# Grouping the numerators of a product-quantised convolution behind its denominators, on one Trainium2 core

## The chip, the cores and the metric

The kernel runs on one core of one Trainium2 chip. The metric is the device time of one execution in microseconds. All times in this text are microseconds unless ns is written. The engines are named as in the profile: PE is TensorE (the matmul array), PEld its weight loads, DVE is VectorE, ACT is ScalarE, POOL is GpSimd, SP is SyncE, which here only issues transfers.

## What is computed

The input x is 16 images of 256 channels, 28 by 28, in fp32. A group norm is followed by two convolutions of 3x3 that are replaced by soft lookups, then by a squeeze-and-excite gate and two residual sums. Cut to what matters:

```python
def amm_conv3x3(x, centroids, w_sub):                  # centroids: (C, 16, 9)
    p = patches_of_3x3(x)                              # B, N, C, 9
    d = sum(p*p) - 2*einsum('bncs,cks->bnck', p, centroids) + sum(centroids**2)
    attn = softmax(-d, axis=-1)                        # over the 16 codes of a channel
    lut = einsum('cks,cso->cko', centroids, w_sub)
    return einsum('bnck,cko->bno', attn, lut)

h = relu(bn1(amm_conv3x3(gn(x), centroids1, wsub1)))   # layer 1
h = bn2(amm_conv3x3(h, centroids2, wsub2))             # layer 2
h = relu(se_layer(h) + gn(x))
return x + h
```

For each pixel and each channel there are 16 logits, a softmax over them, and a weighted sum. The kernel rearranges the sum: it first forms, for each channel and each of the nine taps, the attention-weighted centroid (the numerator, a matmul of the exponentials with the centroids), divides by the sum of the exponentials (the denominator), and multiplies the result q with w_sub (the lookup).

## The kernel before

**Blocks.** An image in one layer is cut into four blocks: two halves of the channels (hh) times two halves of the rows (t), in the order of `BLOCKS`. There are 16 images, 2 layers and so 128 blocks. Block j has four groups of 32 channels, mm = 0 to 3, and 392 pixels.

**What a block does.** `patches` brings nine shifted copies of the padded image from DRAM into one of two tiles `pt`. `logits` (L349) is a matmul in 32x32 tiles of the array, 16 per group mm, into four PSUM banks `lg`; `exps` (L361) takes the exponential of each bank on ScalarE into a tile `e`. `num_b` (L410) makes the denominators and the ninth tap together, in tiles of 64 rows by 32 columns, into two banks `nb`. `split_b` (L421, L423, ScalarE) and `join_b` (L430, L433, VectorE) separate them, `recip_dve` (L436) inverts the denominators, and `spread` (L447, L451) shuffles them to the rows where they are needed, into tiles `rb`. `num_a` (L396) makes the other eight taps, a pair of taps and two banks `na` for each mm. Pairs 0 and 1 are copied out by ScalarE (`copy_a`, L464) and multiplied later by GpSimd (`scale_q`, L459); pairs 2 and 3 are multiplied straight out of PSUM by VectorE (`scale_a`, L470). The ninth tap (the tile `qo`, spread number 4) is scaled by GpSimd as well.

**Lookups.** The lookup of an image is a product of two-by-two blocks (two channel halves in, two out, two row halves), done with seven products instead of eight, in the way of Strassen's scheme. `PRODUCTS` says in which cluster each product runs and with which taps: `KO` is the order of the nine taps, `S1` is split over two clusters. `product` (L478) adds nine 128x128 matmuls into one bank `acc`. The differences of q that the scheme needs are made by GpSimd in `mix` (L485, L487); `acc_copy`, `acc_add` and `reg_add` (L509, L515, L517, L522) put the seven sums together, `norm_out` (L529, L533) applies the batch norm on ScalarE.

**Wide blocks.** In layer 2, blocks of channel half 0 treat their group mm = 0 with a softmax that subtracts the maximum: `wide_copy` (ScalarE, L367), `wide_turn` (a VectorE transpose and a maximum, L372 and L375), `wide_sub` (GpSimd, L381), `wide_back` (VectorE, L385), `wide_exp` (ScalarE, L389).

**The order.** Nothing is left to a scheduler: `at(cl, sub, f, ...)` puts a step into a list under a cluster number and a fraction, and the steps are issued in the order of these two keys; steps under one key go in the order in which they were put. Each engine executes its own steps in that order. Block j has g = 2j. Its logits of mm 0 and 1 are in cluster g, those of mm 2 and 3 in g+1, its denominators in g+2; an image has g = 8n and takes eight clusters. Below, cluster numbers are often taken modulo 8. In an even cluster TensorE does two logits groups of one block, the denominators and numerators 0 and 1 of the block before, and then a lookup (2.0); in an odd cluster two logits groups, numerators 2 and 3, and a lookup.

**Buffers.** PSUM is one ring of eight banks of 2 KiB, shared by all of `lg`, `nb`, `na`, `acc` and a few small sums. An allocation waits until a bank is free. A lookup input lives in one of the tiles `qp` (pairs) or `qo` (ninth taps), whose numbers `NQ` sets and whose use is planned in the list `homes`.

**Other steps that are touched.** Before the first block, channels 0 to 127 and then 128 to 255 of image 0 are normalised (`gn_stats`, `gn_mean`, `gn_var`, `gn_apply`), written to DRAM with `to_home1`, and the codes of layer 1 are centred (`center`: squares by `center_sq`, a matmul and a sum by `center_add`, the subtraction of a mean by `center_mean`). The codes of layer 2 are centred in the same way in clusters 43 to 51 by `prep_wd2` (three parts), `prep_wd3` and `prep_wd4`. `finish_norm`, `finish_gate`, `finish_sum`, `finish_relu` and `finish_add` finish an image of layer 2 in later clusters (3, 4 and 5 of the image after the next).

Of the kernel before, what the change touches and what calls it, by code (L numbers as in the profile page):

```python
# [37 lines left out]
NQ = {"pair": 14, "one": 4}  # L38
# [4 lines left out]
    5: ("A11", 0, KO), 6: ("S1", 0, KO[:3]), 7: ("S1", 0, KO[3:]), 8: ("S3", 1, KO), 9: ("S2", 0, KO),  # L43
# [24 lines left out]
def kernel(  # L68
# [180 lines left out]
    def center_sq(wf, c0, w):  # L249
        sq = rpool.tile([P, N], F32, tag="r", name="sq")  # L250
        nc.vector.tensor_mul(sq[:, :w], wf[:, c0 : c0 + w], wf[:, c0 : c0 + w])
        return sq
# [6 lines left out]
    def center_mean(wf, n):  # L259
        g = wf.rearrange("p (g k) -> p g k", k=K)  # L260
        nc.vector.tensor_reduce(cst[:, : n // K], g, axis=AX.X, op=ALU.add)
        nc.vector.tensor_scalar_mul(cst[:, : n // K], cst[:, : n // K], 1.0 / K)
        nc.vector.tensor_sub(g, g, cst[:, : n // K].unsqueeze(2).to_broadcast([P, n // K, K]))
# [180 lines left out]
    def spread(u, mm):  # L444
        if mm == 4:
            rb = rpool.tile([P, N], F32, tag="rb1", name="rb1", bufs=1)
            nc.vector.stream_shuffle(rb, u["r"], mask_of(8))  # L447
        else:
            rb = rpool.tile([P, 2, N], F32, tag="rb", name="rb", bufs=4)
            for r in range(2):  # L450
                nc.vector.stream_shuffle(rb[:, r, :], u["r"], mask_of(2 * mm + r))  # L451
        u["rb", mm] = rb
# [222 lines left out]
    def prep_wd2(part):  # L675
        pw["sq"] = center_sq(pw["st"][:, 512:1536], 384 * part, min(384, 1024 - 384 * part))
# [4 lines left out]
    def prep_wd4():  # L681
        st = pw.pop("st")
        center_mean(st[:, 512:1536], 1024)
        f = st[:, 512:1536].rearrange("p (g n) -> p g n", n=32)
        nc.vector.tensor_sub(f, f, kbias.unsqueeze(1).to_broadcast([P, 32, 32]))
# [157 lines left out]
    for j, u in enumerate(blocks):  # L843
        gi, g = 8 * (j // 4), 2 * j
        for mm in range(5):
            kind = "one" if mm == 4 else "pair"
            homes.append(((g + 3, 1.1) if 2 <= mm < 4 else (g + 2, 1.4), 1, j, mm, kind))
# [8 lines left out]
    for j, u in enumerate(blocks):  # L856
# [21 lines left out]
        at(g + 2, 1.7, spread, u, 4)  # L878
        at(g + 2, 1.71, scale_q, u, 4)
        for mm in range(2):  # L880
            at(g + 2, 1.35, num_a, u, mm)
            at(g + 2, 1.45, copy_a, u, mm)
            at(g + 3, 1.8, spread, u, mm)
            at(g + 3, 1.8, scale_q, u, mm)
        for mm in range(2, 4):
            at(*((g + 2, 1.8) if mm == 2 else (g + 3, 0.05)), spread, u, mm)
            at(g + 3, 1.0, num_a, u, mm)
            at(g + 3, 1.1, scale_a, u, mm)

    for l in range(2):  # L890
        for b in range(B):
# [3 lines left out]
            for c, (w, r, ks) in PRODUCTS.items():  # L895
                at(g + c, 2.0, product, (n, c), us[r], w, ks)
# [6 lines left out]
            at(g + 6, 0.0, acc_copy, l, b, c11, (n, 5))  # L903
# [14 lines left out]
            if l == 0:  # L918
# [8 lines left out]
                if b + 1 < B:  # L927
                    at(g + (-1 if b else 2), 2.6, load_x, b + 1)
                    for q in range(NB):
                        at(g + (1 + 2 * q if b else 4), 0.3, gn_stats, b + 1, q)  # L930
                    at(g + 4, 1.05 if b else 1.96, gn_mean, b + 1)
                    at(g + 4, 1.33 if b else 1.97, gn_var, b + 1)
                    for q in range(NB):
                        at(g + 5, 0.9, gn_apply, b + 1, q)
                        at(g + 5, 1.9, to_home1, b + 1, q)
# [20 lines left out]
    at(1, 0.6, load_w, 0, "A11")  # L956
    at(3, 0.6, load_w, 0, "S3")
    at(3, 0.6, load_w, 0, "A22")
# [27 lines left out]
    at(51, 0.3, prep_wd4)  # L986
# [20 lines left out]
    for k in range(NB):  # L1007
# [4 lines left out]
        if k == 0:  # L1012
            for i in range(2):
                to_home1(0, 0, i)
            nc.vector.memset(pts[0], 1.0)
            nc.gpsimd.memset(pts[1], 1.0)
    for hh in range(2):
        center(wts["wd", hh].rearrange("p a b c -> p (a b c)"), 512)
    at(-0.5, 0.7, to_home1, 0, 1)
    at(0, 1.95, setup_bn)  # L1020
# [160 lines left out]
```

## Time and profile before

| what | value |
|---|---|
| median of three runs | 2773.61 (2771.26 to 2779.5) |
| profiled execution | 2760.28 |
| its span, as the page counts it | 2758.7 |
| mean granted TensorE clock | 0.987 |
| PE busy | 2674.9 (97%) |
| DVE, ACT, POOL busy | 1732.6, 1454.4, 2066.8 |
| logits L349, matmuls | 533.5 |
| numerators L396, denominators L410 | 412.1, 372.2 |
| lookups L478 from `qp` | 709.0 and 521.3 |
| mixes on POOL, L487 | 938.2 |
| POOL's own scaling, L459 pairs | 473.0 |

The busy times of the page say which engine is occupied. A busy PE is not the same as an array that streams rows: in the timeline, the start of one group of matmuls minus the start of the next shows what a group really costs. In the lists of waits, a line names who waited, for whom, the total, how often, and the longest. In a timeline a line has the start, the duration, the engine, the line of the kernel, the operation, output and inputs, and how many instructions were merged; in square brackets stands the idle time of the engine before it and what ended it.

### The profile page before, as it was taken

The numbers are of one execution on the slowest core, as the hardware profiler recorded it, in microseconds if no ns is written. First come the engines' busy times: TensorE is split into PE (matmuls) and PEld (weight loads), VectorE is DVE, ScalarE is ACT, GpSimd is POOL, SyncE is SP. The second block draws the span as 40 slices with busy tenths as digits, with TensorE's granted clock in tenths as the row PEclk, the third lists the DMA queues.
The fourth block names the chain that finished last, engine by engine and source line by source line (L and its number), as shares of the span: only waits on it lengthen the run. The fifth ranks groups of instructions, "written<-read, shape, count | busy, mean of one in ns | idle before, by whom it ended". The sixth has DMA issues, their size and how long they took to land. (4 is left out here: it accounts for less than half of the span.)

```text
span 2758.7 us, 87946 instructions
## 1 busy us (share of the span) xinstructions
PE 2674.9 (97%) x37076; PEld 1297.7 (47%) x37076; DVE 1732.6 (63%) x3950; ACT 1454.4 (53%) x3277; POOL 2066.8 (75%) x1420
## 2 busy tenths in 40 slices
PE   5989999799999999999999999999999999999997
PEld 2444444344444444444444444444444444444443
DVE  5765555765555565565576766676766666766664
ACT  4444455445455445455455466656566656556653
POOL 4756787738877767766678777888877788877787
PEclk9999999999999999999999999999999999999998
DMA  9665677546677656666585455445555545555541
GB/s 202 149 135 136 165 191 184 146 107 158 154 189 189 157 128 151 158 160 150 117 183 122 105 123 122 111 104 114 114 123 123 115 104 113 116 117 123 117 105 47
DMA packets 223025, 374.51 MB, mean 136 GB/s; under 512 B 30152, under 2 KB 193336, under 8 KB 222624
## 3 DMA queue, kind: packets, MB, share of 16 engines
q1 hardware_dynamic: 215392, 334.50, 53.8%
q0 software_dynamic: 7232, 34.30, 3.6%
q8 instruction: 296, 4.85, 0.8%
q14 instruction: 105, 0.86, 0.1%
HBM read 288.91 MB, written 79.80 MB: 134 GB/s over the span
## 5 line engine op out<-in xcount | busy, mean ns | idle before, releaser
L361 ACT ACTIVATE e<-lg 128x392 f32<-128x392 f32 x1920 | 777.7, 530 | 822.7 <-PE lg L349 821.7
L487 POOL TENSOR_TENSOR qp<-qp,qp 128x784 f32<-128x784 f32 x512 | 938.2, 1862 | 41.8 <-DVE qp L470 41.8
L478 PE MATMUL acc<-qp,w_S 128*128 128x392 f32 x2048 | 709.0, 497 | 5.3 <-POOL qp L487 5.2
L459 POOL TENSOR_TENSOR qp<-qp,rb 128x784 f32<-128x784 f32 x256 | 473.0, 1869 | 253.6 <-DVE rb L451 253.6
L349 PE MATMUL lg<-pt,wd 32*32 32x392 f32 x16384 | 533.5, 503 | 28.8 <-DVE half_sum L515 17.3
L451 DVE STREAM_SHUFFLE rb<-r 128x392 f32<-128x392 f32 x1024 | 550.8, 605 | 0.0
L478 PEld LDWEIGHTS acc<-qp,w_S 128*128 128x128 f32 x2048 | 388.5, 191 | 296.7 <-POOL qp L487 10.9
L478 PE MATMUL acc<-qp,w_A 128*128 128x392 f32 x1536 | 521.3, 493 | 0.0
L396 PE MATMUL na<-e,cwa 64*32 64x392 f32 x8192 | 412.1, 498 | 10.0 <-issue 9.8
L430 DVE SCALAR_TENSOR_TENSOR r<-nb,kst,r 128x392 f32<-128x392 f32 x128 | 79.8, 624 | 517.5 <-ACT r L421 510.6
L478 PEld LDWEIGHTS acc<-qp,w_A 128*128 128x128 f32 x1536 | 292.5, 190 | 213.1
L410 PE MATMUL nb<-e,cwb 64*32 64x392 f32 x8192 | 372.2, 497 | 0.0
L349 PEld LDWEIGHTS lg<-pt,wd 32*32 32x32 f32 x16384 | 230.9, 103 | 282.8 <-issue 179.6
L436 DVE RECIPROCAL r<-r 128x392 f32<-128x392 f32 x128 | 331.9, 2593 | 0.0
L459 POOL TENSOR_TENSOR qo<-qo,rb 128x392 f32<-128x392 f32 x128 | 131.1, 1024 | 220.3 <-DVE rb L447 220.2
L470 DVE TENSOR_TENSOR qp<-na,rb 128x392 f32<-128x392 f32 x512 | 252.4, 555 | 56.1 <-PE na L396 53.1
L396 PEld LDWEIGHTS na<-e,cwa 64*32 64x32 f32 x8192 | 145.2, 106 | 234.6 <-ACT e L361 123.5
L410 PEld LDWEIGHTS nb<-e,cwb 64*32 64x32 f32 x8192 | 146.2, 107 | 209.2 <-issue 126.5
L464 ACT COPY qp<-na 128x392 f32<-128x392 f32 x512 | 211.8, 512 | 10.9 <-PE na L396 10.8
L421 ACT ACTIVATE r<-nb,kst 128x392 f32<-128x392 f32 x128 | 87.5, 684 | 102.3 <-PE nb L410 99.8
L367 ACT COPY e<-lg 128x392 f32<-128x392 f32 x128 | 52.9, 500 | 152.9 <-PE lg L349 152.9
L485 POOL TENSOR_TENSOR qo<-qo,qo 128x392 f32<-128x392 f32 x128 | 130.8, 1022 | 2.2
(143 smaller groups left out, 1778.1 us busy)
## 6 DMA issues: line engine op xcount, KB each, us to landing
pt<-home SPq DMA_DIRECT2D x768, 209.0 KB
pt<-home SPq DMA_DIRECT2D x753, 104.5 KB
home<-xpad SPq DMA_DIRECT2D x31, 899.0 KB
xt<-in_x SPq DMA_DIRECT2D x30, 784.0 KB
out_dram<-y SPq DMA_DIRECT2D x32, 392.0 KB
w_S<-d_wS SPq DMA_DIRECT2D x4, 576.0 KB
st<-in_wsub SPq DMA_DIRECT2D x4, 512.0 KB
st<-d_wa SPq DMA_DIRECT2D x16, 128.0 KB
```

What stands on the lines that cost most here:

```text
L349: nc.tensor.matmul(bk[32 * c : 32 * c + 32, :N].rearrange("p (r w) -> p r w", w=W), lhsT=wts["wd", u["hh"]][32 * i : 32 * i + 32, mm, c, : ...
L361: nc.scalar.activation(eg[:, i, :], bk[:, :N], AF.Exp, scale=2.0)
L396: nc.tensor.matmul(bs[r][32 * i : 32 * i + 32, :N], lhsT=wts["cwa", u["hh"]][64 * r : 64 * r + 64, mm, i, :], rhs=es[64 * r : 64 * r + 64, ...
L410: nc.tensor.matmul(bs[r][32 * i : 32 * i + 32, :N], lhsT=wts["cwb", u["hh"]][64 * r : 64 * r + 64, mm, i, :], rhs=es[64 * r : 64 * r + 64, ...
L436: nc.vector.reciprocal(u["r"], u["r"])
L451: nc.vector.stream_shuffle(rb[:, r, :], u["r"], mask_of(2 * mm + r))
L459: nc.gpsimd.tensor_tensor(q, q, u.pop(("rb", mm)), ALU.mult)
L464: nc.scalar.copy(u["q", 2 * mm + r], bk[:, :N])
L470: nc.vector.tensor_mul(u["q", 2 * mm + r], bk[:, :N], rb[:, r, :])
L478: nc.tensor.matmul(accs[key][:, :N], lhsT=wl[w][:, k, :], rhs=us["q", k], start=first and n == 0, stop=last and n == len(ks) - 1,)
L485: nc.gpsimd.tensor_tensor(out_u["q", 8], in0["q", 8], in1["q", 8], ALU.subtract)
L487: nc.gpsimd.tensor_tensor(pair(out_u, mm), pair(in0, mm), pair(in1, mm), ALU.subtract)
```

## The change

Seven things change.

1. The numerators of all four pairs are issued together right behind the denominators, at 1.31 of cluster g+2. Pairs 2 and 3 leave cluster g+3.
2. The steps behind them are put anew: spreads and products of pairs 2 and 3 (VectorE) at 1.7 of cluster g+2, behind the reciprocal; the spreads of the ninth tap and of pairs 0 and 1, with GpSimd's scaling, at 0.05 of cluster g+3. So an odd cluster has only logits and a lookup on TensorE.
3. The split lookup S1 has eight taps in cluster 6 and one in cluster 7, where it had three and six. The first image's A11 goes to cluster 4.
4. `NQ` has 16 pairs instead of 14, `rb` two buffers instead of four; pairs 2 and 3 get their homes one cluster sooner.
5. The squares, and the two subtractions at the end of the centring of layer 2's codes, go from VectorE to GpSimd; `prep_wd4` goes from 0.3 to 1.9.
6. The head: channels 0 to 127 are normalised first, then half of the codes is centred, then channels 128 to 255 are normalised; the other half of the codes is centred at 1.95 of cluster 0. The first patch tile is set to one in two parts, of which the first half of the tile's groups comes before everything.
7. Some loads and group-norm steps of the next image get other keys.

```diff
-NQ = {"pair": 14, "one": 4}
+NQ = {"pair": 16, "one": 4}
...
-    5: ("A11", 0, KO), 6: ("S1", 0, KO[:3]), 7: ("S1", 0, KO[3:]), 8: ("S3", 1, KO), 9: ("S2", 0, KO),
+    5: ("A11", 0, KO), 6: ("S1", 0, KO[:8]), 7: ("S1", 0, KO[8:]), 8: ("S3", 1, KO), 9: ("S2", 0, KO),
...
-    def center_sq(wf, c0, w):
+    def center_sq(wf, c0, w, eng=None):
         sq = rpool.tile([P, N], F32, tag="r", name="sq")
-        nc.vector.tensor_mul(sq[:, :w], wf[:, c0 : c0 + w], wf[:, c0 : c0 + w])
+        (eng or nc.vector).tensor_mul(sq[:, :w], wf[:, c0 : c0 + w], wf[:, c0 : c0 + w])
...
-        nc.vector.tensor_sub(g, g, cst[:, : n // K].unsqueeze(2).to_broadcast([P, n // K, K]))
+        (eng or nc.vector).tensor_sub(g, g, cst[:, : n // K].unsqueeze(2).to_broadcast([P, n // K, K]))
...
-            rb = rpool.tile([P, 2, N], F32, tag="rb", name="rb", bufs=4)
+            rb = rpool.tile([P, 2, N], F32, tag="rb", name="rb", bufs=2)
...
-        pw["sq"] = center_sq(pw["st"][:, 512:1536], 384 * part, min(384, 1024 - 384 * part))
+        pw["sq"] = center_sq(pw["st"][:, 512:1536], 384 * part, min(384, 1024 - 384 * part), nc.gpsimd)
...
-        center_mean(st[:, 512:1536], 1024)
+        center_mean(st[:, 512:1536], 1024, nc.gpsimd)
         f = st[:, 512:1536].rearrange("p (g n) -> p g n", n=32)
-        nc.vector.tensor_sub(f, f, kbias.unsqueeze(1).to_broadcast([P, 32, 32]))
+        nc.gpsimd.tensor_sub(f, f, kbias.unsqueeze(1).to_broadcast([P, 32, 32]))
...
-            homes.append(((g + 3, 1.1) if 2 <= mm < 4 else (g + 2, 1.4), 1, j, mm, kind))
+            homes.append(((g + 2, 1.4), 1, j, mm, kind))
...
-        at(g + 2, 1.7, spread, u, 4)
-        at(g + 2, 1.71, scale_q, u, 4)
+        for mm in range(4):
+            at(g + 2, 1.31, num_a, u, mm)
+        for mm in range(2, 4):
+            at(g + 2, 1.7, spread, u, mm)
+            at(g + 2, 1.7, scale_a, u, mm)
+        at(g + 3, 0.05, spread, u, 4)
+        at(g + 3, 0.05, scale_q, u, 4)
         for mm in range(2):
-            at(g + 2, 1.35, num_a, u, mm)
             at(g + 2, 1.45, copy_a, u, mm)
-            at(g + 3, 1.8, spread, u, mm)
-            at(g + 3, 1.8, scale_q, u, mm)
-        for mm in range(2, 4):
-            at(*((g + 2, 1.8) if mm == 2 else (g + 3, 0.05)), spread, u, mm)
-            at(g + 3, 1.0, num_a, u, mm)
-            at(g + 3, 1.1, scale_a, u, mm)
+            at(g + 3, 0.05, spread, u, mm)
+            at(g + 3, 0.05, scale_q, u, mm)
...
-                at(g + c, 2.0, product, (n, c), us[r], w, ks)
+                at(g + c - (c == 5 and n == 0), 2.0, product, (n, c), us[r], w, ks)
...
-            at(g + 6, 0.0, acc_copy, l, b, c11, (n, 5))
+            at(g + (6 if n else 5), 0.0, acc_copy, l, b, c11, (n, 5))
...
-                    at(g + (-1 if b else 2), 2.6, load_x, b + 1)
+                    at(*((g - 1, 2.6) if b else (2, 1.65)), load_x, b + 1)
...
-                    at(g + 4, 1.05 if b else 1.96, gn_mean, b + 1)
-                    at(g + 4, 1.33 if b else 1.97, gn_var, b + 1)
+                    at(g + 4, 1.05 if b else 2.1, gn_mean, b + 1)
+                    at(g + 4, 2.2, gn_var, b + 1)
                     for q in range(NB):
-                        at(g + 5, 0.9, gn_apply, b + 1, q)
-                        at(g + 5, 1.9, to_home1, b + 1, q)
+                        at(g + 5, 0.9 if b else 0.3, gn_apply, b + 1, q)
+                        at(g + 5, 1.9 if b or q else 0.9, to_home1, b + 1, q)
...
-    at(1, 0.6, load_w, 0, "A11")
-    at(3, 0.6, load_w, 0, "S3")
-    at(3, 0.6, load_w, 0, "A22")
+    at(1, 1.65, load_w, 0, "A11")
+    at(3, 1.65, load_w, 0, "S3")
+    at(3, 1.65, load_w, 0, "A22")
...
-    at(51, 0.3, prep_wd4)
+    at(51, 1.9, prep_wd4)
...
-    for k in range(NB):
+    def norm0(k):
         gn_stats(0, k)
         gn_mean(0, k, 1)
         gn_var(0, k, 1)
         gn_apply(0, k)
-        if k == 0:
-            for i in range(2):
-                to_home1(0, 0, i)
-            nc.vector.memset(pts[0], 1.0)
-            nc.gpsimd.memset(pts[1], 1.0)
-    for hh in range(2):
+
+    def center_wd(hh):
         center(wts["wd", hh].rearrange("p a b c -> p (a b c)"), 512)
+
+    nc.vector.memset(pts[0][:, :4], 1.0)
+    norm0(0)
+    for i in range(2):
+        to_home1(0, 0, i)
+    nc.vector.memset(pts[0][:, 4:], 1.0)
+    nc.gpsimd.memset(pts[1], 1.0)
+    center_wd(0)
+    norm0(1)
+    at(0, 1.95, center_wd, 1)
     at(-0.5, 0.7, to_home1, 0, 1)
-    at(0, 1.95, setup_bn)
+    at(0, 1.96, setup_bn)
```

More of the change, by code (lines that the diff above doesn't have):

```diff
@@ L257, in center_add, with center_mean @@
         nc.vector.tensor_add(wf[:, c0 : c0 + w], wf[:, c0 : c0 + w], ps[:, :w])
-    def center_mean(wf, n):
+    def center_mean(wf, n, eng=None):
         g = wf.rearrange("p (g k) -> p g k", k=K)
```

## The prediction

> **What bounds the kernel now.** I read the page's busy times first, then the array's own waits, then the order of time in two stretches: one block of layer 1, and the passage between two clusters of layer 2. A cluster is one step of the job list; cluster numbers below are taken modulo 8 (eight per image, two per block), layer 1 and 2 are the two convolutions.
>
> ```profile
> PE 2674.9 (97%) x37076; PEld 1297.7 (47%) x37076; DVE 1732.6 (63%) x3950; ACT 1454.4 (53%) x3277; POOL 2066.8 (75%) x1420
> ```
>
> TensorE is busy 97% of 2758.7 us and idles 84. So only two things can move the time: array time that isn't rows streamed, and new waits of the array. Its own waits are few and mostly happen once:
>
> ```profile
> PE lg L349 <- DVE half_sum L515: 17.3, 2, 15.4
> PE lg L349 <- DMA pt<-home: 8.8, 3, 6.6
> PE acc L478 <- POOL qp L487: 5.2, 6, 3.5
> ```
>
> The columns are total us, times, longest. Now one block in order of time (start, duration), the reader should subtract starts:
>
> ```profile
> 622.49 2.06 PE L349 MATMUL lg<-pt,wd 32*32 32x392 f32 x64
> 623.42 3.23 ACT L361 ACTIVATE e<-lg 128x392 f32<-128x392 f32 x8 [0.29 <-PE lg L349]
> 624.48 2.86 PE L410 MATMUL nb<-e,cwb 64*32 64x392 f32 x64
> 627.14 1.52 PE L396 MATMUL na<-e,cwa 64*32 64x392 f32 x32
> 627.43 0.68 ACT L421 ACTIVATE r<-nb,kst 128x392 f32<-128x392 f32 x1 [0.79 <-PE nb L410]
> 628.57 1.64 ACT L464 COPY qp<-na 128x392 f32<-128x392 f32 x4
> 628.59 0.93 PE L478 MATMUL acc<-qo,w_S 128*128 128x392 f32 x2
> 629.26 2.59 DVE L436 RECIPROCAL r<-r 128x392 f32<-128x392 f32 x1
> ```
>
> Start to start: half the logits 1.99, denominators (64 instructions) 2.66, half the numerators (32) 1.45. In the other half-block the numerators stand alone between logits and lookups: 632.72 to 634.22 and 614.80 to 616.37, 1.50 and 1.57; the median of 111 such stages is 1.57. Full lookups take 6.12 (18 instructions), 12 take 4.15 and 6 take 2.17: 0.33 each plus 0.19. These medians hold almost everywhere: in steady state the array does not wait. Even clusters last 1.95+2.66+1.45+6.12 = 12.2, odd ones 1.95+1.57+6.12 = 9.6.
>
> Last, layer 2 from cluster 3 into 4, where ScalarE is full:
>
> ```profile
> 2078.94 2.03 PE L349 MATMUL lg<-pt,wd 32*32 32x392 f32 x64
> 2082.95 1.59 ACT L389 ACTIVATE e<-e 128x1568 f32<-128x1568 f32 x1
> 2086.22 1.84 ACT L777 ACTIVATE y<-y,se_gt 128x784 f32<-128x784 f32 x2
> 2088.58 2.03 PE L349 MATMUL lg<-pt,wd 32*32 32x392 f32 x64
> 2089.51 3.23 ACT L361 ACTIVATE e<-lg 128x392 f32<-128x392 f32 x8
> 2090.54 2.86 PE L410 MATMUL nb<-e,cwb 64*32 64x392 f32 x64
> 2093.24 1.66 ACT L793 ACTIVATE y<-y 128x784 f32<-128x784 f32 x2
> 2094.73 0.73 ACT L421 ACTIVATE r<-nb,kst 128x392 f32<-128x392 f32 x1
> ```
>
> The exponentials of 2089.51 start with no idle before them, 0.93 after their logits, exactly as in an unloaded block: ScalarE is just in time here, with nothing to spare.
>
> **What the Trainium skill says.** "TensorEngine Tiling (Array Packing)", Key Properties: changing the tiling mode drains the array. The trace agrees: 32 numerator instructions cost 1.33 (half of 2.66) inside a 64-row group, 1.57 alone. "PSUM — Partial Sum Buffer", Specifications: eight banks. The pool has exactly these eight, and the trace shows an array waiting 15.4 for one bank behind half_sum. "SBUF — State Buffer", SBUF: two separate sides: VectorE with two SBUF inputs and GpSimd take a shared port pair exclusively. The trace agrees once, harshly: a 128x256 squaring on VectorE (0.42 four times in the head) took 16.7 while GpSimd ran without a gap.
>
> **The change, part by part.** Sums are against the profiled execution, 2760.3 (span 2758.7 and 1.6 around it); the runs' median, 2773.6, is 13.3 above it, so I add the difference to the median.
>
> *A. One switch less.* The numerators of pairs 2 and 3 leave the odd cluster (1.57 saved) and join the group (1.33 added): 0.24 x 128 blocks = **-30.7**. The odd cluster then goes from 32-row logits straight to 128-row lookups. That junction isn't in the trace with lookups; logits followed by the 128-row group-norm matmul take 1.96, so I price it as unchanged. Bounds: no saving at all (0) to -40.
>
> *B. A bank for the fourth pair.* Denominators (2 banks) and four pairs (8) need ten banks of eight. The fourth pair can start only when split_b has freed one and a copy another. The array wants it 2.66+3x0.665 = 4.66 after the denominators' start; the first copy ends at 628.57+0.51-624.48 = 4.60, and in the head a weight load followed such a copy by 0.1. So about 0.1 late, 114 blocks: **+11**. Queued behind it: the lookups. Bounds: 0, and 51 if it gets join_b's bank instead (629.34-624.48 = 4.86, plus 0.1: 0.3 in 96 blocks; 0.7 in the 32 whose VectorE first does wide_turn).
>
> *C. Clusters 6, 7, 8.* Lookups split 8+1 instead of 3+6: same total, but cluster 6 must outlast the new VectorE chain. Join ends 6.75 after the cluster's start, reciprocal to 9.5, then two shuffles and two products per pair, 1.0 each: the last bank is free at 13.4, and the next logits start at 1.95+2.66+2.78+5.46 = 12.85, needing it at 14: covered. But cluster 7 shrinks to 1.95+0.85 = 2.8 (3.3 in layer 2), while ScalarE needs 3.23 for each cluster's exponentials: it is 0.43 late in layer 1, 0.3 in layer 2. The denominators need the first two banks these free, and have no slack (0.93+0.41+0.53+0.1 = 1.97 against 1.95). 16x0.43+15x0.3 = **+11** (0 to 20).
>
> *D. Layer 2, cluster 3 to 4.* The odd cluster is 8.07 instead of 9.64, so cluster 4 comes 1.57 sooner. And wide_exp (L389) comes later: it waits for wide_back on VectorE, which now stands behind the pair-3 product (ends 13.95, an odd cluster starts at 13.5), an accumulation (0.5), and the five shuffles of 0.5 that moved to 0.05: 16.95 to 18.7, or 5.2 after the cluster's start where 2082.95-2078.94 = 4.0 stood. From wide_exp to the next exponentials ScalarE has 6.56 of work (2082.95 to 2089.51): they start at 11.8, wanted at 8.07+0.93 = 9.0: 2.8 late, and the denominators wait 2.8. Then norm_out and finish_relu (2.2, to 2094.73) stand ahead of split_b: the exponentials' last start plus 2.2 gives split_b 4.2 after the denominators' start instead of 2.95, the first copy ends 1.2 late, and the fourth pair waits 1.4 (B). 4.2 for each of the 14 images with finishing work: **+59** (0 if something hides it, 75).
>
> *E. Layer 2, cluster 9.* GpSimd's scale_q of pairs 0 and 1 now starts after the pair-3 product, 14.1 after cluster 6's start, GpSimd being idle from about 10; scales 4.7, mixes 8.4, wide_sub 2.85, mixes again 8.4 (from rows of 7.32 for four and 1.0): 38.4. The lookups of cluster 9 start near 32.2 (12.85+3.3 for clusters 6 and 7, 13.5+0.3+0.2 for cluster 8, 1.95 of logits) and want their last pair 4.8 later (0.19+14x0.33), at 37.0: they wait about **1.5**, 15 times: **+23** (0 to 30). In layer 1 wide_sub is absent and they fit by 0.6.
>
> *F. Centring of layer 2's codes on GpSimd.* Gone: the 16.7 squaring with its 15.4 wait, and about 2 of slow array after it (nb took 4.97): -19. New: part 2's squaring stands on GpSimd behind the scales (end 18.8 after cluster 6's start), three mixes (4.7) and itself (0.7, as L738's 128x256): ready at 24.3, where the array wants it in cluster 8 at 18.0: +6.3 once. Parts 0 and 1 fall behind scales only and are ready in time. prep_wd4's two subtractions find GpSimd idle. **-13** (-19 to 0).
>
> *G. Small.* The array's 5.2 of waits on mixes: scales come earlier in most clusters, **-5**. Head: VectorE does 1.43 of memset, 6.0 of centring, then the second half's norm (3.3) before GpSimd's four norm operations (1.65), behind which its patch transfers stand: 21.0 instead of 16.3; landing takes 5.7 to 6.9, so the first logits run near 28 instead of 24.7. Given back: the 5.2 wait on gn_dv is covered by the lookups moved to cluster 4, and the array idles less before cluster 2, during which the granted clock was 0.5 (from 36 to 40). **0**, -4 to +4. Other moves (load_x, load_w on SP, gn_apply, buffers rb 4 to 2, qp 14 to 16) have users at least a cluster later: nothing; without that cover, one landing of some 8.
>
> Sum: -30.7+11+11+59+23-13-5 = **+55**; profile 2816, median **2829**.
>
> **Rivals.**
> *Faster (0.17).* The saved switch decides. Place: every odd cluster, 0.24 each, plus F and G: -49. It wins as long as B to E together stay under 49, 0.38 per block; with C at its price and D and E hidden, -37: 2737 (2725 to 2748). For it: medians equal to minima in almost all stages. Against: the exponentials at 2089.51 without idle.
> *Fourth pair waits for join_b (0.13).* B is 51: 2869. For it: the order of frees is a compile-time choice the trace can't show.
> *No saved switch (0.08).* Logits to lookups costs what the lone numerators cost: 2860. Against: 1.96 before the group-norm matmul.
> *Even (0.12).* wide_exp keeps its place, so D is 2.0 (1.6 and 0.4) x 14 = 28, and E is hidden: -30.7+11+11+28-18 = +1: 2775.
>
> **How the numbers follow.** My case has 0.50. Runs of before span 0.3%, which is about what can be told from no change. Faster: the first rival and a quarter of the even one, 0.20; within 0.3%: 0.07; slower: 0.73. Range: up to the bank rival with some spare, 2875; down to the upper end of the faster one, 2745; about 0.12 is left below and 0.07 above.
>
> **What would show it.** Right: odd clusters of 8.1 and even ones of 13.5 in layer 1, denominators and numerators 5.4 to 5.6 together; in layer 2, denominators starting 4 to 5 after the logits in cluster 4, with ScalarE without idle before; lookups of cluster 9 waiting on mixes; no 16.7 squaring. Wrong: layer 2 as regular as layer 1 (then the first rival), or a standing gap within the group (the bank rival).

## The result and the profile after

The changed kernel takes 2880.35 (median of four runs, 2874.25 to 2890.56) where the kernel before, run beside it, takes 2773.21 (2771.26 to 2779.5): a ratio of 1.0386, 95% interval 1.0348 to 1.0424. It is slower by about 107; the prediction said 2829, slower by 56, with a range that ended at 2875. The direction was foretold, the size was half of it. The profiled execution took 2875.7, its span is 2874.2 against 2758.7: 115.5 to be explained.

The first line of the page, as before with busy times and shares:

```profile
PE 2714.6 (94%) x37076; PEld 1339.4 (47%) x37076; DVE 1719.6 (60%) x3945; ACT 1458.0 (51%) x3278; POOL 2072.2 (72%) x1425
```

TensorE has the same 37076 matmuls, but is idle for 160 instead of 84, and busy 40 longer. Where it waits over the whole execution (who, for whom, total, times, longest):

```profile
PE lg L349 <- DMA pt<-home: 40.9, 16, 4.7
PE nb L410 <- ACT e L361: 28.9, 15, 2.2
...
PE lg L349 <- ACT y L509: 9.7, 14, 2.6
...
PE acc L478 <- POOL qp L487: 5.4, 18, 1.3
```

The first three lines are new or grown, and nearly all of their time is in layer 2, about once per image: 12 of the 16 waits for patches with 31.7 of the 40.9, and all but one or two of the others. The wait for mixes, 5.2 before, is what it was. A block of layer 1 is as foretold (start and duration; in this and the later timelines, rows of other steps are left out):

```profile
823.13 2.16 PE L349 MATMUL lg<-pt,wd 32*32 32x392 f32 x64
825.22 2.86 PE L410 MATMUL nb<-e,cwb 64*32 64x392 f32 x64
827.87 2.86 PE L396 MATMUL na<-e,cwa 64*32 64x392 f32 x64
830.66 0.93 PE L478 MATMUL acc<-qo,w_S 128*128 128x392 f32 x2
...
836.79 2.02 PE L349 MATMUL lg<-pt,wd 32*32 32x392 f32 x64
838.74 0.93 PE L478 MATMUL acc<-qo,w_A 128*128 128x392 f32 x2
```

Start to start, denominators and all four pairs take 830.66 - 825.22 = 5.44, and logits go into lookups in 1.95.

The most useful view is one that the page doesn't have: the length of each cluster, from the first logits of one to the first logits of the next, taken from the timeline. Means over fifteen images, clusters modulo 8; the kernels are explained below:

| layer 2 | 0 | 1 | 2 | 3 | 4 | 5 | 6 | 7 | image |
|---|---|---|---|---|---|---|---|---|---|
| before | 12.21 | 9.64 | 12.23 | 9.65 | 12.19 | 9.91 | 8.37 | 8.17 | 82.4 |
| changed | 14.93 | 8.34 | 13.57 | 8.08 | 16.98 | 8.34 | 14.36 | 5.47 | 90.1 |
| e1 add first | 16.73 | 8.34 | 13.57 | 8.08 | 17.04 | 8.34 | 12.88 | 3.31 | 88.3 |
| e2 store late | 16.07 | 8.34 | 13.57 | 8.09 | 17.18 | 8.34 | 16.32 | 3.31 | 91.2 |
| e3 ScalarE relieved | 15.37 | 8.34 | 13.57 | 8.08 | 14.24 | 8.34 | 14.02 | 5.72 | 87.7 |
| e4 both | 16.50 | 8.34 | 13.57 | 8.08 | 14.27 | 8.34 | 12.88 | 3.31 | 85.3 |
| e5 gate later | 13.93 | 10.02 | 16.07 | 8.08 | 14.17 | 8.34 | 12.89 | 2.81 | 86.3 |
| e12 addition on ScalarE | 14.40 | 9.07 | 13.57 | 8.08 | 14.23 | 8.34 | 12.91 | 3.31 | 83.9 |
| e9 gate split | 13.72 | 9.79 | 13.57 | 8.08 | 14.23 | 8.34 | 12.87 | 3.31 | 83.9 |
| e10 wide_back first | 13.72 | 9.76 | 13.57 | 8.08 | 13.64 | 8.34 | 12.89 | 3.31 | 83.3 |
| e13 mixes early | 13.72 | 8.08 | 13.57 | 8.08 | 13.62 | 8.34 | 12.87 | 3.31 | 81.6 |

Layer 1, fifteen images together: 1295.4 before, 1282.4 changed. So of the 115.5, the head has +5.3, layer 1 -13.0, fifteen images of layer 2 +115.7, the last image and the end +7.5. In row e13 the array is idle for only 1.4 in all fifteen images; against it the changed kernel loses, in the mean over the images, 1.2 in cluster 0, 3.4 in cluster 4, 1.5 in cluster 6 and 2.2 in cluster 7.

Not all of this is waiting. In these fifteen images the array is idle for 75.9 in the changed kernel and for 0.4 before, and the record of the granted clock stands at one half for 75.1 and before at no time. Half of the 75.1, some 37, is an estimate of what the clock adds: about a third of the 115.7. By the cluster in which a stretch of low clock starts, these are 23.9 in cluster 4, 6.8 in cluster 6, 27.3 in cluster 7 and 17.1 in cluster 0, which are the clusters with waits.

Cluster 4 was foretold (term D). The passage from cluster 3, in order of time:

```profile
2128.15 2.10 PE L349 MATMUL lg<-pt,wd 32*32 32x392 f32 x64
2133.66 1.51 ACT L389 ACTIVATE e<-e 128x1568 f32<-128x1568 f32 x1 [1.29 <-DVE e L385]
2136.30 2.02 PE L349 MATMUL lg<-pt,wd 32*32 32x392 f32 x64
2140.01 3.16 ACT L361 ACTIVATE e<-lg 128x392 f32<-128x392 f32 x8
2140.54 2.91 PE L410 MATMUL nb<-e,cwb 64*32 64x392 f32 x57 [2.21 <-ACT e L361]
2145.23 0.70 ACT L421 ACTIVATE r<-nb,kst 128x392 f32<-128x392 f32 x1
2146.55 1.26 PE L396 MATMUL na<-e,cwa 64*32 64x392 f32 x16 [0.79 <-ACT qo L423]
```

The wide exponential starts 5.5 after cluster 3, the exponentials start 3.7 after their logits instead of 0.93 and without idle of ScalarE before them, the denominators wait 2.21 and the fourth pair 0.79.

Clusters 6 and 7 were not foretold. The same image a little later:

```profile
2155.12 1.03 POOL L459 TENSOR_TENSOR qo<-qo,rb 128x392 f32<-128x392 f32 x1 [13.53 <-DVE rb L447]
2156.20 3.66 POOL L459 TENSOR_TENSOR qp<-qp,rb 128x784 f32<-128x784 f32 x2
2159.81 3.67 POOL L796 TENSOR_TENSOR y<-y,xt 128x784 f32<-128x784 f32 x2
2161.69 2.15 SPq L807 DMA_DIRECT2D out_dram<-y  x2
2163.93 1.47 SPq L335 DMA_DIRECT2D pt<-home  x1
2164.14 0.49 ACT L509 COPY y<-acc 128x392 f32<-128x392 f32 x1 [1.56 <-DMA out_dram<-y]
```

and in the kernel before, where cluster 5 starts at 2100.77:

```profile
2100.99 3.68 POOL L796 TENSOR_TENSOR y<-y,xt 128x784 f32<-128x784 f32 x2
```

`finish_add` (L796) and the moved scalings have the same key, 0.05 of an odd cluster, and the scalings were put into the list first. So the add, which came 0.2 after the start of cluster 5, now comes 6.0 after it (2159.81 - 2153.86), behind three scalings for which GpSimd idled 13.5. SP's queue holds the store of that y, and behind the store the patches of cluster 7, `load_x`, and the patches of cluster 8. SP's wait for the add (first line: before, second: changed kernel) nearly doubles:

```profile
SPq L807 <- POOL y L796: 183.5, 29, 45.6
```

```profile
SPq L807 <- POOL y L796: 343.6, 29, 51.7
```

GpSimd's lateness is thus handed to transfers with which it has nothing to do; and `acc_copy` in cluster 6 wants a y buffer that is still being stored.

### The profile page after: what moved, and what is told of

It is laid out like the page before. It is cut to its first block, busy times and chain, and to the rows that moved or that the text cites. A ratio compares the mean times of both kernels' runs of the same rounds, so it can differ in the third digit from the quotient of the medians.

```text
span 2874.2 us, 88051 instructions
## 1 busy us (share of the span) xinstructions
PE 2714.6 (94%) x37076; PEld 1339.4 (47%) x37076; DVE 1719.6 (60%) x3945; ACT 1458.0 (51%) x3278; POOL 2072.2 (72%) x1425
## 5 line engine op out<-in xcount | busy, mean ns | idle before, releaser
L349 PE MATMUL lg<-pt,wd 32*32 32x392 f32 x16384 | 566.2, 517 | 72.0 <-DMA pt<-home 40.9
L410 PE MATMUL nb<-e,cwb 64*32 64x392 f32 x8192 | 403.0, 521 | 32.1 <-ACT e L361 28.9
L396 PE MATMUL na<-e,cwa 64*32 64x392 f32 x8192 | 389.3, 494 | 10.7 <-ACT qo L423 5.5
L349 PEld LDWEIGHTS lg<-pt,wd 32*32 32x32 f32 x16384 | 237.9, 104 | 337.2 <-issue 213.0
L410 PEld LDWEIGHTS nb<-e,cwb 64*32 64x32 f32 x8192 | 160.2, 112 | 262.2 <-issue 131.4
L396 PEld LDWEIGHTS na<-e,cwa 64*32 64x32 f32 x8192 | 170.4, 107 | 202.4 <-issue 95.0
L470 DVE TENSOR_TENSOR qp<-na,rb 128x392 f32<-128x392 f32 x512 | 261.6, 553 | 0.0
L541 POOL DMA_INDIRECT home<-hpad,col x60 | 61.2, 1021 | 103.1 <-ACT hpad L529 74.0
```

The costliest lines, as they stand in the source:

```text
L349: nc.tensor.matmul(bk[32 * c : 32 * c + 32, :N].rearrange("p (r w) -> p r w", w=W), lhsT=wts["wd", u["hh"]][32 * i : 32 * i + 32, mm, c, : ...
L396: nc.tensor.matmul(bs[r][32 * i : 32 * i + 32, :N], lhsT=wts["cwa", u["hh"]][64 * r : 64 * r + 64, mm, i, :], rhs=es[64 * r : 64 * r + 64, ...
L410: nc.tensor.matmul(bs[r][32 * i : 32 * i + 32, :N], lhsT=wts["cwb", u["hh"]][64 * r : 64 * r + 64, mm, i, :], rhs=es[64 * r : 64 * r + 64, ...
L470: nc.vector.tensor_mul(u["q", 2 * mm + r], bk[:, :N], rb[:, r, :])
```

## The experiments

Three or four kernels were run at a time on one chip with the kernel before beside them. Its medians were 2771.4 for e1 to e4, 2757.1 for e5 to e8, 2772.3 for e9 to e12 and 2758.4 for e13 to e15, so whole times are compared between these sets by the ratios; where a kernel is called so many microseconds faster or slower than another, this is the difference of ratios times 2773. None leaves out any of the computation. The first theory, Q, is the reading above: the add's place in GpSimd's queue costs about 4.9 per image, beside D. Its first rival, S, has ScalarE's overload in cluster 4 alone as the cause, handed on to the clusters behind.

**e1, the add first.** One key of the changed kernel.

```diff
-                        at(g + 21, 0.05, finish_add, b, q)
+                        at(g + 21, 0.04, finish_add, b, q)
```

> The changed kernel with one key altered: finish_add stands ahead of the moved scalings in GpSimd's queue (0.04 instead of 0.05), as in the kernel before. Theory Q (queue): in layer 2 the residual add stood behind three scalings that wait for the end of the lookups, and store and patch transfers on SP stood behind the add; the copy of y in cluster 6 (1.3 to 1.5), the patches of cluster 8 (2.15) and the slower clock after that idle (1.4) all go, about 4.9 for each of 14 images: -68, near 2812 (1.014 of the kernel before), and no cluster-8 wait on patches is left. Rival S (ScalarE): the lateness of clusters 6 to 8 is handed on from the overload in cluster 4: the time stays within 10 of 2880.

Measured: ratio 1.0272 (1.0249 to 1.0296), some 32 less than the change's 1.0386, where 68 were expected. Clusters 6 and 7 are at 12.88 and 3.31, where they stay (but for 2.81 once) in all kernels of the table that have this edit, so theory Q names the right cause for them, and S falls. But cluster 0 grew from 14.93 to 16.73: of the 3.65 per image that went, 1.8 came back there. Something else was late in cluster 0 and had been hidden by the wait for patches.

**e2, the store late.**

```diff
-                        at(g + 21, 0.06, store, b, q)
+                        at(g + 21, 0.7, store, b, q)
```

> The changed kernel with the store put behind the patch transfers of cluster 7 in SP's queue (0.7 instead of 0.06); the add stays behind the scalings. Theory Q splits: the patches no longer wait, so cluster 7's and cluster 0's share (2.15 and 1.4) goes, about -48, near 2832, while the copy of y in cluster 6 still waits for the store to land (1.3 each, 18 in all). If the y buffer were the whole of it (rival Y), the time stays within 10 of 2880; if the store, load_x and the patches of cluster 8 only crowd each other later (rival C), between -10 and -30.

Measured: 1.0468 (1.0436 to 1.0499), no gain but a loss of some 23. The patches of cluster 8 are in time (cluster 7 at 3.31), as Q says. The store, now behind patches, lands later still, and ScalarE's wait for the y buffer (first line: changed kernel, second: e2) doubles:

```profile
ACT y L509 <- DMA out_dram<-y: 20.5, 13, 2.0
```

```profile
ACT y L509 <- DMA out_dram<-y: 38.8, 14, 4.0
```

Cluster 6 rises by 2.0, cluster 0 by 1.1. The forecast of -48 failed: a jam that is let past at one place stands at the next. The order on GpSimd has to be mended, not the order on SP.

**e3, ScalarE relieved.**

```diff
-                        at(g + 19, 0.91, finish_gate, b, q)
+                        at(g + 18, 1.75, finish_gate, b, q)
...
-                        at(g + 20, 0.9, finish_relu, b, q)
+                        at(g + 20, 1.75, finish_relu, b, q)
```

> The changed kernel with ScalarE relieved between clusters 3 and 4 of layer 2: finish_gate moved to the end of cluster 2 (ScalarE idles 6.8 there), finish_relu moved behind cluster 4's bank copies. Term D of the prediction: cluster 4 falls from 17.0 to about 14.3 (gate 1.77 ahead of the exponentials, relu 1.62 ahead of split_b; wide_exp still stands late): -2.7 x 14 = -38, near 2842. Rival W: it is wide_back's place on VectorE alone that makes it late, so under -10. Rival M (masked): the gain in cluster 4 is given back in clusters 5 to 7, where the store's chain is pinned to the end of the lookups: -10 to 0.

Measured: 1.0209 (1.0179 to 1.024), some 49 less where 38 were expected. Cluster 4 falls by 2.74 to 14.24, as expected to a tenth. Term D is right in mechanism and place. M and W fall.

**e4, both edits.**

> Both edits, the add first and ScalarE relieved. If the two are separate costs they add: -106, near 2774 (1.000 of the kernel before). If one hides behind the other, no better than the better of the two alone plus 10 (2800 to 2840).

Measured: 1.0115 (1.0093 to 1.0138), some 75 less than the change; the two single gains were 32 and 49. They add, within the intervals, but the sum expected had e1's 68 in it. What is left stands in cluster 0 (16.50). There (e4, start and duration):

```profile
2056.10 3.23 ACT L361 ACTIVATE e<-lg 128x392 f32<-128x392 f32 x8 [0.39 <-PE lg L349]
2059.13 0.48 ACT L768 ACTIVATE se_gt<-sep,nb_sb 128x1 f32<-128x1 f32 x2
2059.65 1.35 DVE L771 TENSOR_SCALAR se_gt<-se_gt 128x2 f32<-128x2 f32 x1 [1.48 <-ACT se_gt L768]
2061.11 0.55 DVE L515 TENSOR_TENSOR half_sum<-acc,half_sum 128x392 f32<-128x392 f32 x1
2061.72 0.86 PE L349 MATMUL lg<-pt,wd 32*32 32x392 f32 x8 [1.19 <-DVE half_sum L515]
2062.51 4.56 PE L410 MATMUL nb<-e,cwb 64*32 64x392 f32 x64
```

The chain reads upwards: the denominators take 4.34 to the next start instead of 2.66; before them the last eight logits matmuls waited for a bank; the bank is freed by `half_sum`; VectorE executes `half_sum` behind `se_gate`'s addition (L771), which waits for ScalarE's exponentials of the gate, which stand behind the exponentials of cluster 7. Cluster 7 used to last 8.2 and had room for this; with eight of nine lookups moved to cluster 6 it lasts 3.3. Second, an addition over 128x2 took 1.35; in the changed kernel it had already taken 1.34 in the median. The view of that line, in the kernel before and in e5 below (minimum, median and maximum in ns):

```profile
L771 DVE TENSOR_SCALAR se_gt<-se_gt x16: 168/169/171, 1546.8 to 2748.3; 128x2 f32<-128x2 f32 x16
```

```profile
L771 DVE TENSOR_SCALAR se_gt<-se_gt x16: 170/6014/6196, 1558.4 to 2800.1; 128x2 f32<-128x2 f32 x16
```

Third, the clock. By stretches of e4, an undisturbed one and two behind the wait (the last four columns: POOL busy, granted clock, DMA share, GB/s):

```profile
2042.00:2047.00 5.00, 5.00 (x145) 2.50 (x152) 0.00 (x0) 3.84 (x10) 5.00 (x4) 1.00 0.95 227
2062.00:2064.50 2.50, 2.50 (x41) 0.87 (x41) 2.47 (x2) 0.84 (x2) 2.50 (x2) 0.74 0.70 151
2064.50:2067.00 2.50, 2.50 (x48) 1.17 (x40) 0.69 (x1) 0.00 (x0) 2.50 (x2) 0.58 0.94 189
```

0.74 and 0.58 are means over these stretches. The clock record itself has one stretch at one half, 3.41 long, from 2063.18 to 2066.59, and full clock on both sides. It begins 1.5 after the end of the wait, and 4.34 - 2.66 = 1.7, half of 3.41, are lost to it. In layer 2 of e4 thirteen waits of 1.0 to 1.2 occur in cluster 0; nine were followed by such a stretch and four were not. What decides is not shown.

**e5, the gate later.** On top of e4, `se_gate` goes to cluster 1.

```diff
-                at(g + (14 if last else 15), 1.05, se_gate, b)
+                at(g + (14 if last else 17), 1.05, se_gate, b)
```

> The kernel with both edits (add first, ScalarE relieved), and se_gate of layer 2 moved from the short cluster 7 to cluster 1 (key g+17). Theory H: cluster 7 now lasts 3.3 instead of 8.2, so se_gate's exponentials stand behind its exponentials on ScalarE, its VectorE steps wait for them, and half_sum behind those steps frees cluster 8's eighth bank late; the logits stretch from 1.95 to 4.1 and the denominators after that idle run at a lower clock (4.34 instead of 2.66). Cluster 8 falls from 16.5 to about 13.9, its length in the two images without finishing work: -2.6 x 14 = -36, near 2767. Rival E (the prediction's term E, late mixes on GpSimd): the wait moves on to the lookups of cluster 9, and no more than 10 is gained. Rival K (the low clock comes with the layer, not with the wait): -1.2 x 14 = -17, near 2787, and the denominators stay at 4.3.

Measured: 1.0228 (1.0208 to 1.0248), slower than e4 by about 31 where it was expected to be faster by 36. Yet cluster 0 fell to 13.93 with denominators of 2.66, just as theory H says, and K falls. The loss is new: clusters 1 and 2 rose by 1.7 and 2.5.

```profile
1990.35 7.31 POOL L487 TENSOR_TENSOR qp<-qp,qp 128x784 f32<-128x784 f32 x4
1996.18 6.08 DVE L771 TENSOR_SCALAR se_gt<-se_gt 128x2 f32<-128x2 f32 x1 [1.94 <-ACT se_gt L768]
1997.58 1.05 POOL L459 TENSOR_TENSOR qo<-qo,rb 128x392 f32<-128x392 f32 x1
1998.55 3.68 POOL L459 TENSOR_TENSOR qp<-qp,rb 128x784 f32<-128x784 f32 x2
2002.37 1.02 DVE L515 TENSOR_TENSOR y<-acc,y 128x392 f32<-128x392 f32 x2
2003.44 0.86 PE L349 MATMUL lg<-pt,wd 32*32 32x392 f32 x8 [2.29 <-DVE y L515]
```

The addition over 128x2 starts inside a run of GpSimd work and ends at 2002.26, when that run ends (1998.55 + 3.68 = 2002.23). "SBUF — State Buffer", "SBUF: two separate sides", in the Trainium skill says that VectorE, in a two-port mode or with two SBUF inputs, shares a port pair with GpSimd, and that whichever starts first holds it for one whole instruction while the other blocks. This addition has one SBUF input; in which mode it ran no run here shows. The trace agrees on the blocking. In e4 the addition ends at 2061.00, with the GpSimd instruction during which it started (2060.97), as the page says. Here it doesn't: three more GpSimd instructions follow without a gap, and the addition ended only behind the last of them. That the port pair is the cause is read from these times, not measured by itself. In e5 nine of the sixteen additions took 6.0 to 6.2 and six 1.2 to 1.8; what decides between the two is not shown. The squaring of 16.7 in the kernel before is of this kind too: GpSimd worked without a gap until 551.97, the squaring ended at 552.25. The accumulation of y stands behind it, a bank behind that, and in eight of the fifteen images the low clock again (cluster 2 lasts 18.2 to 18.3 there, and 13.6 in the others).

**e6, the scalings back.** The changed kernel with one part undone.

```diff
-        at(g + 3, 0.05, spread, u, 4)
-        at(g + 3, 0.05, scale_q, u, 4)
+        at(g + 2, 1.71, spread, u, 4)
+        at(g + 2, 1.71, scale_q, u, 4)
...
-            at(g + 3, 0.05, spread, u, mm)
-            at(g + 3, 0.05, scale_q, u, mm)
+            at(g + 3, 1.8, spread, u, mm)
+            at(g + 3, 1.8, scale_q, u, mm)
```

> The changed kernel with one part undone: shuffles and scalings of pairs 0, 1 and of the one go back to their keys of before (1.8 of the odd cluster and 1.7); group, split of the lookups and all else stay. Theory Q: the add and the store are in front again, and wide_back no longer stands behind five shuffles, so ScalarE's wide_exp comes 2 earlier: clusters 6 and 7 as with the add first (12.9, 3.3), cluster 4 about 15 instead of 17; cluster 8 still 16.5 to 17.3 by se_gate. About -31 - 2 x 14 = -59, near 2821. Rival E: the pairs of cluster 5 are scaled a cluster later, mixes come later, and lookups of clusters 6 and 9 wait for them by 1 to 2 each: no better than 2850.

Measured: 1.0398 (1.0379 to 1.0416), the same as the change, where 59 less were expected. Clusters 6 and 7 go to 12.92 and 3.32 and cluster 4 to 15.70, as theory Q says, but cluster 0 rises to 18.15 and layer 1 to 1294.4. In cluster 7 the four shuffles at 1.8 now stand between the gate and `half_sum` on VectorE, and `half_sum` starts 3.9 after cluster 8's logits. Why layer 1 grows by 12 was not followed. The rival's bound (2850) held, in layer 2 for another reason than its own.

**e7, the centring alone,** put into the kernel before.

> The kernel before with term F alone: squarings and subtractions of layer 2's code centring on GpSimd, prep_wd4 at 1.9. The prediction says -19 for the squaring's wait and the slow array behind it, +6.3 where the third squaring stands behind mixes: -13 (2758, ratio 0.995). Rival: the squaring's 16.7 was a wait for a shared port that some other VectorE step now suffers in its place: 0 (ratio 0.999 to 1.001).

Measured: 0.9955 (0.9939 to 0.997), -12.5, or -17 to -8 by the interval; term F's -13 lies in its middle. The squaring of layer 2's codes, before and in e7:

```profile
L251 DVE TENSOR_TENSOR sq<-st x3: 1508/1510/16732, 493.8 to 535.5; 128x384 f32<-128x384 f32 x2, 128x256 f32<-128x256 f32 x1
```

```profile
L251 POOL TENSOR_TENSOR sq<-st x3: 607/822/827, 492.0 to 535.7; 128x384 f32<-128x384 f32 x2, 128x256 f32<-128x256 f32 x1
```

On GpSimd it takes 0.6 to 0.8. The third, alike on both but for the engine, had taken 16.7 on VectorE.

**e8, the old head** in the changed kernel.

> The changed kernel with the head of the kernel before (order of norm, centring, memsets, loads and the first product's place). The trace of the changed kernel has cluster 8 start 5.3 later than before. If the new head itself is slower: start of cluster 8 near 91 and -5, near 2875. If the lateness comes from the group and the moved scalings instead: start near 96, and no change.

Measured: 1.0415 (1.0398 to 1.0433), no gain, and cluster 8 starts at 95.9. In e7, whose head is that of before, it starts at 94.7 against 91.2. So the start of cluster 8 moves by some 3 without any edit of the head, and 5.3 is no clear cost of the new one. Term G's "0" for the head is not contradicted.

**e9, the gate split,** on top of e4; and **e12**, only its addition on ScalarE, nothing moved.

```diff
 # e9
-        nc.vector.tensor_scalar_add(gt, gt, 1.0)
-        nc.vector.reciprocal(gt, gt)
         se[b] = gt
+    def se_recip(b):
+        gt = se[b]
+        nc.scalar.activation(gt, gt, AF.Copy, bias=1.0)
+        nc.vector.reciprocal(gt, gt)
...
+                at(*((g + 14, 1.06) if last else (g + 16, 1.65)), se_recip, b)
 # e12
-        nc.vector.tensor_scalar_add(gt, gt, 1.0)
+        nc.scalar.activation(gt, gt, AF.Copy, bias=1.0)
```

> The kernel with add first and ScalarE relieved, and se_gate split: its exponentials stay in cluster 7, the addition of 1 goes to ScalarE and stands with the reciprocal at 1.65 of cluster 8, behind half_sum. Theory H with the port: the addition on VectorE (128x2, 0.17 in the kernel before) took 1.35 in cluster 7 and 6.0 in cluster 1 while GpSimd worked without a gap; without it in front, half_sum is in time, the logits of cluster 8 take 1.95, the denominators 2.66, and cluster 1 and 2 stay at 8.1 and 13.6. Ratio 1.0115 - 0.013 = 0.9985 of the kernel before. Rival E: mixes on GpSimd are late behind it all the same, cluster 8 stays above 15: 1.007 to 1.012.

> The kernel with add first and ScalarE relieved, where the addition of 1 in se_gate runs on ScalarE in place, in cluster 7, and nothing is moved. If the 1.35 of the addition on VectorE is what makes half_sum late (port), half_sum comes 1 earlier, the wait of 1.2 goes, and with it the low clock: cluster 8 near 14.2, -2.3 x 14 = -32, ratio 1.000. If it is the place behind ScalarE's exponentials (queue), the reciprocal still waits for them, half_sum comes at most 0.8 earlier, the array still waits and the clock still falls: ratio 1.008 to 1.0115.

Measured: e9 1.0022 (1.0015 to 1.0029), e12 1.003 (1.002 to 1.0039), 26 and 24 less than e4 where 36 and 32 were expected. Cluster 0 went to 13.72 and 14.40. Since the addition alone, left in its place, brings nearly all of it, the addition's long run on VectorE, read above as the wait for the port, counted for more than its place in the queue. In e12 the array has no wait over 0.63 in these images and the clock record is never below full there. The rest of the expected gain shows up in cluster 1: 9.79 and 9.07 instead of 8.34. That is term E of the prediction, come out from behind the other waits.

**e10, wide_back first,** on top of e9, and **e11**, lookups 7+2 on top of e10.

```diff
 # e10
-                    at(g + 1, 0.3, wide_back, u, mm)
+                    at(g + 1, 0.04, wide_back, u, mm)
 # e11
-    ... 6: ("S1", 0, KO[:8]), 7: ("S1", 0, KO[8:]), ...
+    ... 6: ("S1", 0, KO[:7]), 7: ("S1", 0, KO[7:]), ...
```

> As the split gate, and wide_back (VectorE) ahead of the five shuffles (0.04 instead of 0.3 of the odd cluster). The rest of term D: cluster 4 of layer 2 lasts 14.2 with ScalarE relieved where 13.5 is undisturbed; wide_exp comes some 2.5 earlier, -0.7 x 14 = -10: 0.995. If the last 0.7 is norm_out ahead of the exponentials (rival N), no change to the split gate (0.9985).

> As wide_back first, with the lookups of clusters 6 and 7 split 7+2 instead of 8+1. Term C said that cluster 7 is too short for ScalarE's 3.23 of exponentials by 0.43 in layer 1 and 0.3 in layer 2; in the trace cluster 8 of layer 1 lasts 13.8 against 13.5. With 7+2 the cluster lasts 3.15, and that 0.3 x 30 = 8 goes: 0.992. Rival: the fourth pair's bank is now late at cluster 7's logits (needed at 13.35, free at 13.4 or later), and the sum of clusters 6 to 8 stays or grows: 0.995 to 1.0.

Measured: e10 0.9989 (0.998 to 0.9998), e11 0.9985 (0.9976 to 0.9993). Cluster 4 falls from 14.23 to 13.64: the rest of D, worth 9 as expected. With 7+2, clusters 6, 7 and 0 of layer 2 sum to 29.92 in both: nothing. Cluster 1 stays at 9.76 in both, and there the lookups wait (e10):

```profile
2143.15 7.29 POOL L487 TENSOR_TENSOR qp<-qp,qp 128x784 f32<-128x784 f32 x4
2148.70 1.58 PE L478 MATMUL acc<-qp,w_S 128*128 128x392 f32 x4 [0.23 <-POOL qp L487]
2150.50 1.58 PE L478 MATMUL acc<-qp,w_S 128*128 128x392 f32 x4 [0.21 <-POOL qp L487]
```

The lookups run in step with the mixes, one pair every 1.8.

**e13, mixes early,** on top of e10; **e14**, `prep_cwa` on ScalarE besides; **e15**, the changed kernel with nothing but the mixes moved.

```diff
 # e13, e15
-                at(g + 7, 2.5 if mm < 2 else 1.75, mix, us[1], mm, us[2], us[1])
+                at(g + 7, {2: 0.04, 3: 0.04, 4: 1.75}.get(mm, 2.5), mix, us[1], mm, us[2], us[1])
 # e14
-            nc.vector.tensor_scalar(f[...], src[...], m_cw[:, c : c + 1], None, op0=ALU.mult)
+            nc.scalar.activation(f[...], src[...], AF.Copy, scale=m_cw[:, c : c + 1])
```

> As wide_back first, and the mixes of pairs 2 and 3 into block 1 (key g+7) ahead of the scalings of pairs 0 and 1 in GpSimd's queue, where GpSimd idles some 8 in cluster 6. Term E: with the other waits gone, the lookups of cluster 9 wait 1.65 for mixes in each image of layer 2; GpSimd's chain starts 2 earlier, so cluster 1 falls from 9.7 to 8.1: -1.65 x 15 = -25, ratio 0.9989 - 0.009 = 0.990. If the 1.65 is not the mixes' lateness but something that stands ahead of them (the half-sum additions on GpSimd at cluster 0), no change: 0.997 to 1.000.

> As mixes early, and the four scalings of prep_cwa (once, in cluster 53) on ScalarE instead of VectorE, where they took 14.4 for four of 128x256 while GpSimd worked. If this stands in the array's way (cluster 54 lasts 16 to 17.7 against 13), -3 to -5: 0.9885. If the cluster is long for another reason, 0.990 and cluster 54 unchanged.

> The changed kernel with only the mixes moved. If term E is masked there (the array reaches cluster 9 late in any case, cluster 1 lasts 8.1 to 8.3), nothing in layer 2 changes: within 6 of 2880, ratio 1.036 to 1.040. If E is a cost of its own in the changed kernel, -25: 1.0295.

Measured: e13 0.9878 (0.9861 to 0.9896), e14 0.9873 (0.9855 to 0.9892), e15 1.0347 (1.0327 to 1.0367). In e13 cluster 1 is at 8.08 in every image of layer 2, the 1.65 is gone, and the fifteen images take 1223.8 instead of 1249.5 in e10, the 25 expected:

```profile
2109.60 7.33 POOL L487 TENSOR_TENSOR qp<-qp,qp 128x784 f32<-128x784 f32 x4
2113.03 0.93 PE L478 MATMUL acc<-qo,w_S 128*128 128x392 f32 x2
2113.79 5.43 PE L478 MATMUL acc<-qp,w_S 128*128 128x392 f32 x16
```

In e15 layer 2 as a whole doesn't move (1349.8 against 1351.2): there E is masked. Layer 1 takes 1267.6 instead of 1282.4, but no run shows that this comes from the mixes: cluster 1, where lookups would wait for them, lasts 8.17 there instead of 8.20, the array's waits for mixes in layer 1 of the changed kernel are 2.2 in all, and layer 1 takes 1275.1 in e5 and 1277.0 in e8, in which no mix was moved. The whole of e15 came out a little under the 1.036 to 1.040 expected, with an interval that overlaps that of the changed kernel (1.0348 to 1.0424). e14 shortens cluster 54, with its 14.4 of `prep_cwa`, from 17.7 to 14.5, which is under what the total can tell. Both e13 and e14 beat the kernel before, by some 34, as does e7 by 12.5; between e13 and e14 there is nothing to choose.

## Why the prediction was half right

Point by point, in its own letters.

*A, one switch less (-30.7): right.* Clusters 2 and 3 together last 21.65 in layer 2 and 21.73 (medians) in layer 1, against 21.88 and 21.96: 0.23 per block, 0.24 foretold. In e13, with the waits gone, fifteen images of layer 2 take 1223.8 against 1235.5, so 11.7 of the 14.4 foretold for their 60 blocks is there.

*B, the fourth pair's bank (+11): right in kind, less in size.* Cluster 2 is 13.57 where the stages sum to 1.95 + 2.66 + 2.79 + 6.12 = 13.52. Cluster 2 shows no wait for join_b's bank, so that rival is out there. In cluster 4 of layer 1 the four pairs take 3.22 in the mean in the changed kernel, but 2.81 in e8 and e15; why was not followed.

*C, cluster 7 too short (+11): the place was right, the mechanism wrong.* ScalarE's exponentials cost little; a split of 7+2 changed nothing. What the short cluster lost was the cover for `se_gate`, which the prediction didn't put on its list. In the changed kernel cluster 0 has lost 1.2 by this and by the wait for patches; with that wait gone, 3.0 (e1), of which the half clock is some 1.4 (41.0 at half in fifteen images).

*D, ScalarE between clusters 3 and 4 (+59): right.* Measured 3.36 x 15 = 50; 2.74 of the 3.36 go with the gate and the relu moved, 0.6 with wide_back. The prediction made more of wide_back's place than there is.

*E, mixes for cluster 9 (+23): right in mechanism, and hidden.* In layer 2 0.26 in the changed kernel, 1.7 in e9 and e10, 1.5 foretold. The array came to cluster 9 late for other reasons. In layer 1 it was put at nothing, and no run shows a cost there.

*F, centring on GpSimd (-13): right,* -12.5 alone. The new wait for the third squaring is there, 5.9 in the changed kernel where 6.3 was foretold, and 3.3 in e7.

*G, small: the head right within what can be seen; the -5 of mixes didn't come* (5.2 before, 5.4 after).

**The step that failed** is in the list of moves itself. D followed the moved shuffles through VectorE's queue and E the moved scalings into the mixes; for the rest, G ended in "nothing". No term asked which step stands next behind the scalings in GpSimd's own queue. `finish_add` had key 0.05 all along; it came first as long as the scalings had 1.8. That is 1.49 + 2.16 = 3.65 x 15 = 55 in clusters 6 and 7 of the changed kernel. With the 18 (1.2 x 15) of cluster 0, less the 9 by which D was too dear and the 19 of E that stayed masked, it makes 45. The profiled execution, from which these figures come, took 2875.7 where 2816 was forecast, 60 more: the 45 are most of it, and the rest lies in the head, layer 1 and the last image and is not assigned to a step.

The costs don't add. Removing the add's lateness from the changed kernel gave 32 of its 55, because the gate was late behind it; removing that showed E. What stays open: why the low clock follows some of these waits and not others of the same length, and what makes the start of cluster 8 differ by 3 to 5 between executions. Layer 1 stays open too. The saved switches and F alone would give 1295.4 - 14.4 - 19.9 = 1261 (19.9 is the difference between the single traces of before and e7); the changed kernel takes 1282 and e13 1267. Some clusters 6 of e13 still last 15 to 21 there instead of 12.9, and that was not followed further.

## What to carry to other kernels

When a step gets a new place in a hand-written order, list what stands directly behind that place on the same engine, equal keys included, and follow it through the queues: here GpSimd's lateness went through a store on SP to transfers that feed TensorE. When a cluster is shortened, ask of each small step in it what covers it now. After one wait is removed, measure again before counting the next gain: three waits lay one behind the other here, and only with all of them gone (e13) did the new order beat the kernel before by more than the centring alone (e7). It needed no new work, only other places in the order and one addition on another engine.

## What the runs showed of the hardware

- A VectorE addition over 128x2 took 0.17 with GpSimd idle (before), 1.35 when it ended with the GpSimd instruction during which it had started (e4), and 6.08 when it ended only with a run of four of them (e5). The reciprocal of the same 128x2, also on VectorE, took 0.17 while GpSimd worked.
- The array's clock fell after short waits: in e4 nine of thirteen waits of 1.0 to 1.2 were followed by a half clock for 3.41 (once for twice that), four were not, and with the wait gone (e12) the clock stayed full in layer 2. The Trainium skill, "TensorE: Matmul & The Clock Gate", "Part 1: The HAM clock gate (the "warmup" mystery)", has the clock fall after an idle window of about 3.4; here, in e4, the longest wait before such a stretch was 1.2, about a third of that.
- A reordering of SP's queue let patches past a store and made the kernel slower by 23 (e2): ScalarE's waits for the landing of the store, whose buffer it needs, went from 20.5 to 38.8.
